# Order of work at the start of expert and mixer stages, and sums of squares folded over blocks before TensorE

## The chip, the cores and the metric

The kernel runs on one core of a Trainium2 chip. The metric is the device time of one execution in microseconds (us), here of the one core's program; the time before is the median of three runs. Engines are named as in the profile: PE (TensorE products; PEld its weight loads), DVE (VectorE), ACT (ScalarE), POOL (GpSimd), SP (SyncE). Each engine runs its own queue of instructions, and waits for others by semaphores. A suffix "q" (ACTq, SPq) marks an instruction that only issues a DMA.

## The reference

A model of four layers on 1,024 tokens of width 256, taken as two batches of 512. Each layer is half a feed-forward part, a mixing part, and half a feed-forward part again:

```python
x = x + 0.5 * ffn(layernorm(x))
x = x + attn(layernorm(x))
x = x + 0.5 * ffn(layernorm(x))
```

The feed-forward parts of layers 0 and 3 are mixtures of experts (32 experts with 6 per token, and 8 experts with 2 per token). Cut to what matters:

```python
scores = softmax(x @ router.T)            # layer 3: sigmoid
w, idx = top_k(scores, K); w = w / (sum(w) + 1e-20)
ye  = (silu(xe @ w_gate) * (xe @ w_up)) @ w_down     # xe: an expert's tokens
y   = sum over the K chosen experts of w * ye
sh  = (silu(x @ ws_gate) * (x @ ws_up)) @ ws_down    # shared expert
return y + sh
```

The mixing parts of layers 2 and 3 are selective state-space mixers (8 heads and 64 heads of width 64, a state of 128, a short convolution of 4 taps):

```python
z, xBC, dt = split(x @ in_proj)
x, B, C = split(silu(conv4(xBC)))
dt = softplus(dt + dt_bias); dA = dt * -exp(A_log)
y[t] = sum_{s<=t} C[t].B[s] * exp(cum[t]-cum[s]) * dt[s] * x[s] + D * x[t]
y = y * silu(z)
y = y * rsqrt(mean(y*y) + eps) * norm_w
return y @ out_proj
```

## The kernel before, in words

The program runs ten stages one after the other: l0_ffn, l0_attn, l0_ffn, l1, l2_ffn, l2_attn, l2_ffn, l3_ffn, l3_attn, l3_ffn. The running x stays in SBUF, tokens on the partitions, 8 chunks of 128 tokens, 4 (CB) to a batch. The order on each engine is set at build time by a scheduler, which takes the program's instructions, their dependencies and its own estimates; `in_order` (L135) chains the instructions traced inside it, engine by engine, so that the listed engines keep the written order. `evac` (L126) copies PSUM to SBUF alternately on DVE (L130) and ACT (L132).

**A MoE stage** (`moe`, four calls: layer 0 twice, layer 3 twice). For each batch: `layernorm` (xn, L223 on DVE), the rows of xn to a table in HBM by a DMA that ACT issues (L652), eight transposes on PE (L177) whose results are evacuated into xT. Then `logits` (ps_lg L317 on PE, lg L320 on DVE), the scores (softmax in layer 0, L728; sigmoid in layer 3, L744), `topk` on DVE (L299 to L309; tk_gt L309 is the mask) and `slot_lists` (L413 on): running sums over tokens by PE (ps_pos L427, L428, from sl_pre and tk_gt), sl_full (L437), sl_v (L441), integer pieces (sl_vi, sl_hl), two one-hot arrays (sl_ol, sl_oh, L459 and L465), their 64 small products (ps_sl L473), a transposition (ps_slt L493), and sl_put and sl_get (L502, L503): for every slot of every expert, which row it takes. A second DMA of ACT puts the weights of the tokens in the table (L672). Traced after this, and allowed on PE only after the logits, is the shared expert (`shared_unit` L354): per batch, two blocks of gate and up products (pg, pu, L365), s = silu (ACT, L368), h = s * pu (DVE, L369), 16 products acc (L375), two additions to x (DVE, L393). The in_order of the front names PE alone.

`experts_sparse` then goes over the units (an expert with up to two tiles of 128 slots): gathers by POOL (L527, table rows at sl_get; four units ahead), `turn_x` (4 transposes, 2 for one tile, L541, evacuated as xeT), `hidden` (ps_gu L551, silu se L555 on ACT, he L556 on DVE), `turn_h` (L565), `down_` (ps_ye L576), and an indirect write of the rows by POOL (L581). In each pass n of its loop (L607 to L620) it traces turn_x(n), turn_h(n-2), hidden(n-1), down_(n-2), so at the start turn_x(0), turn_x(1), hidden(0).

**A mixer stage** (`mamba`; layer 2 has one group of 8 heads, layer 3 has eight). A unit is a batch and a group; a step is one of its four chunks. For a unit there are four blocks of 128 channels: `conv` makes pp on PE (L1675), scales it on ACT (L1678), and gives back its taps (three DVE instructions, L1682) and its SiLU (ACT, L1686) as separate parts; `prep_back` transposes the block (pt L1757) and evacuates it (xt L1758). For a chunk, lm holds the decays of all heads: a DMA brings rows in, `exponents` adds terms on DVE (8 instructions, L1785), `raised` takes one Exp over two chunks on ACT (L1790), `masked` multiplies by the mask M (DVE, L1794). `z_gate` is pz on PE and its SiLU (L1809, L1817), `main` is py on PE (L1837), `gate` is y on DVE and POOL (L1863, L1864), `squares` adds y*y into sqs, 128 channels x 4 blocks x 128 tokens to a chunk (ACT L1871, in later groups ACT L1874 and POOL L1875), `project` is yacc on PE (L1882), `new_state` is pst on PE (L1852) with ACT or DVE (L1854, L1856). When a batch is through, `add_row` sums the squares over channels with products against a column of ones (pr L1896: for each of the 4 chunks, 4 blocks accumulated; the profile counts 32 because each fp32 product stands in two passes), takes rs on ACT and DVE (L156, L157), and adds yacc times rs to x (L1907). For the first batch this falls between the first step of the second batch and its new_state; for the second it ends the stage. ACT needs another table for Exp, Ln, SiLU and Sqrt.

The mixer's start (from about L1950) is an order written out by hand under in_order for PE, ACT and DVE: batch 0's layernorm, decays (`decay_sums`, a generator whose parts are taken with next; d0 and d1 for the two batches: Exp and Ln of dt, dA, jb), the convolutions, the four blocks x[0] to x[3] (x[i][0]() is the taps, x[i][1]() the SiLU), the first exponents and the first Exp, and then the loop over steps. In layer 2 (`few`) batch 1's layernorm and decays stand in the start; in layer 3 they are spread over the first steps.

Of the kernel before, what the change touches and what calls it, by code (L numbers as in the profile page):

```python
# [83 lines left out]
class Net:  # L84
# [421 lines left out]
    def experts_sparse(self, ew, ps, xes, table, rows, lists, w, ex, f, tiles, per, ahead=4, wp=None):  # L506
# [100 lines left out]
        for n in range(N + 2):  # L607
            if n + ahead < N:
                fetch(n + ahead)
            if n < N:  # L610
                st[n].append(turn_x(n, st[n][1], len(units[n][1])))
            if 0 <= n - 2 < N:
                st[n - 2].append(turn_h(n - 2, st[n - 2][3], len(units[n - 2][1])))
            if 0 <= n - 1 < N:
                (wgu, _), xe, xeT = st[n - 1][:3]
                e, js = units[n - 1]
                st[n - 1].append(hidden(n - 1, e, xe, xeT, wgu, len(js)))
            if 0 <= n - 2 < N:
                down_(n - 2, *units[n - 2], st[n - 2][4], st[n - 2][0][1])
                del st[n - 2]  # L620

    def moe(self, pre, names, E, F, K, FS, PER, tiles, cap, r, scores, scale):
# [6 lines left out]
        with ExitStack() as es:  # L629
            lists = es.enter_context(tc.tile_pool(name="f0li", bufs=1))  # L630
            table = self.dram.tile([T, RW], F32, name=f"table{self.calls}")
            rows = self.dram.tile([r * T, D], F32, name=f"rows{self.calls}")
            rv = rows.rearrange("(c p n) d -> c p n d", p=P, n=r)
            xes = [lists.tile([P, 2, RW], F32, name=f"xe{i}") for i in range(6)]
            for t in xes:
                nc.gpsimd.memset(t, 0.0)
            with ExitStack() as fs:
                psA = fs.enter_context(tc.tile_pool(name="f0a", bufs=2, space=PSUM))
                psM = fs.enter_context(tc.tile_pool(name="f0m", bufs=4, space=PSUM))
                psL = fs.enter_context(tc.tile_pool(name="f0l", bufs=2, space=PSUM))  # L640
                xT = fs.enter_context(tc.tile_pool(name="xT", bufs=1)).tile([P, KD, T], F32, name="xT")
                work = fs.enter_context(tc.tile_pool(name="f0w", bufs=2))
                sb = fs.enter_context(tc.tile_pool(name="f0", bufs=1))
                with tc.tile_pool(name="ln", bufs=1) as lp:
                    tv = table[:, :D].rearrange("(b c p) d -> b p c d", p=P, b=B)
                    rT = self.router_weights(sb, psM, router, E)
                    tail = {}
                    with self.in_order(tail, ("PE",)):
                        for b in range(B):
                            xn = lp.tile([P, CB, D], F32, name=f"xn{b}")  # L650
                            self.layernorm(lp, xn, b, *self.scales(lp, b))
                            nc.scalar.dma_start(tv[b], xn)  # L652
                            for k in range(KD):
                                self.transpose_tokens(xn, xT, psM, b, k)
                        s = self.logits(sb, psM, xT, rT, E)
                if cap < T:

                    zero = lists.tile([P, D], F32, name="zero")
                    nc.vector.memset(zero, 0.0)
                    for c in range(NC):  # L660
                        nc.gpsimd.dma_start(rv[c, :, :K, :], zero.unsqueeze(1).to_broadcast([P, K, D]))
                m = sb.tile([P, NC], F32, name="m")
                scores(s, m)
                mask = self.topk(sb, s, E, K)
                get, put, full = self.slot_lists(lists, sb, psL, mask, E, PER * P, cap, r)
                nc.vector.tensor_tensor(s, s, mask, ALU.mult)
                nc.vector.tensor_reduce(m, s, AX.X, ALU.add)
                nc.vector.tensor_scalar(m, m, 1e-20, None, ALU.add)
                nc.vector.reciprocal(m, m)
                nc.vector.tensor_scalar(m, m, scale, None, ALU.mult)  # L670
                nc.vector.tensor_tensor(s, s, m.unsqueeze(2).to_broadcast([P, NC, E]), ALU.mult)
                nc.scalar.dma_start(table[:, D:].rearrange("(c p) e -> p c e", p=P), s)  # L672
                blocks = self.load_shared(sg, su, sd, FS)
                with tc.issue_after(tail["PE"]):
                    for half in range(B):
                        self.shared_unit(work, psA, psM, xT, blocks, half, 0.5)
                over = lists.tile([1, 1], I32, name="over")
                nc.vector.tensor_scalar(over, full[0:1, :], float(len(tiles) * P), None, ALU.is_gt)
            ew = es.enter_context(tc.tile_pool(name="f0e", bufs=1))
            with tc.tile_pool(name="f0p", bufs=1, space=PSUM) as psE:  # L680
                self.puts = []
                args = (table, rows, (get, put), (wg, wu, wd), list(range(E)), F)
                self.experts_sparse(ew, psE, xes, *args, tiles, PER)
            self.prepare_next()
            with tc.tile_pool(name="f0q", bufs=1, space=PSUM) as psE:
                some = nc.values_load(over[0:1, 0:1], min_val=0, max_val=1)
                wp = es.enter_context(tc.tile_pool(name="f0o", bufs=3))
                with tc.If(some > 0):
                    rest = list(range(len(tiles), -(-cap // P)))
                    self.experts_sparse(ew, psE, xes, *args, rest, PER, ahead=0, wp=wp)  # L690
# [871 lines left out]
    def mamba(self, pre, win, wout, nh):  # L1562
# [14 lines left out]
        with ExitStack() as es:  # L1577
# [166 lines left out]
            def prep_front(u, m):  # L1744
                wo, g = u["wo"], u["g"]
                taps, silu = conv(u["wx"][:, :, m * P : (m + 1) * P], g * NM + m, u["b"], u["xc"][:, m, :])

                def rest():
                    nc.scalar.mul(wo[:, m, :], wo[:, m, :], nw[:, g * NM + m : g * NM + m + 1])
                    silu()  # L1750

                return taps, rest
# [27 lines left out]
            def exponents(k):  # L1780


                for h in range(HG):
                    n = k["u"]["g"] * HG + h
                    nc.vector.scalar_tensor_tensor(  # L1785
                        k["lm"][:, h, :], k["lm"][:, h, :], jb[:, k["c"], n : n + 1], top, ALU.add, ALU.min
                    )
# [78 lines left out]
            def squares(k):  # L1866
# [5 lines left out]
                else:  # L1872
                    sq = wk.tile([P, GC], F32, tag="sq", name="sq")
                    nc.scalar.activation(sq, yf, AF.Square)  # L1874
                    nc.gpsimd.tensor_tensor(sqs[:, cc, :], sqs[:, cc, :], sq, ALU.add)  # L1875

            yacc = [psA.tile([P, 2, D], F32, name=f"yacc{i}") for i in range(CB // 2)]

            def project(k):
# [11 lines left out]
            def add_row(b):  # L1891

                pr = psM.tile([P, CB], F32, tag="mm", name="pr")
                for cc in range(CB):
                    for m in range(NM):
                        nc.tensor.matmul(  # L1896
                            pr[:, cc : cc + 1],
                            sqs[:, cc, m * P : (m + 1) * P],
                            self.ones[:, 0:1],
                            start=(m == 0),  # L1900
                            stop=(m == NM - 1),
                        )
                rs = wk.tile([P, CB], F32, tag="rs", name="rs")
                self.rsqrt(rs, pr, scale=1.0 / DI)
                for cc in range(CB):
                    xc = self.x[:, b * CB + cc, :]
                    nc.vector.scalar_tensor_tensor(  # L1907
                        xc, yacc[cc // 2][:, cc % 2, :], rs[:, cc : cc + 1], xc, ALU.mult, ALU.add
                    )
# [27 lines left out]
            with self.in_order(tail, ("PE", "Activation", "DVE")):  # L1937
# [36 lines left out]
                x[1][1]()  # L1974
                x.append(prep_front(us[0], 2))
                prep_back(us[0], 0)
                exponents(ks[0])
                x[2][0]()
                x[2][1]()
                prep_back(us[0], 1)  # L1980
                x.append(prep_front(us[0], 3))
                exponents(ks[1])
                x[3][0]()
                if few:
                    next(d1)
                    next(d1)
                raised(ks[0])
                prep_back(us[0], 2)
                if few:
                    next(d1)  # L1990
                x[3][1]()
                back = (us[0], NM - 1)
                if few:
                    later = {0: [d1.__next__, d1.__next__, d1.__next__], 1: [d1.__next__, lambda: next(d1, None)]}
# [6 lines left out]
            for s in range(NS):  # L2001
# [4 lines left out]
                with self.in_order(tail):  # L2006
# [30 lines left out]
                    if cc % 2 == 0 and ahead:  # L2037
                        exponents(ks[s + 2])
                    if s > 0:
                        project(ks.pop(s - 1))  # L2040
                if s > 0 and n and cc == 0 and order[n][1] == 0:
                    add_row(order[n - 1][0])
                with self.in_order(tail):
# [6 lines left out]
                    elif last and cc == CB - 1:  # L2050
                        products(1)
            squares(ks[NS - 1])
            project(ks.pop(NS - 1))
            add_row(B - 1)

# [63 lines left out]
```

## Time and profile before

| | us |
|---|---|
| median of three runs | 2031.36 (2030.21 to 2033.29) |
| the profiled execution | 2029.85 |
| its span | 2028.0 |
| PE busy | 1762.7 |
| DVE busy | 1131.6 |
| POOL busy | 903.5 |
| ACT busy | 800.6 |
| first gather of the four MoE calls (the wait for sl_get L503 ends just before) | 72.6, 497.9, 1204.3, 1935.3 |

How to read it: the span runs from the first to the last instruction of the profiled execution, whose own time is 1.85 us longer. A line of the timeline gives the start, the duration, the engine and line, the operation with its result and operands, the shape, how many instructions are taken together, and in brackets the idle time of the engine before it and what ended it. Rows of one line that follow each other closely are taken together, so a row's duration can overlap that of the next. The slices cut the span into 40 parts of 50.7 us; PEclk is the granted PE clock in tenths. The mean granted clock of the execution was 0.917.

### The profile page before, as it was taken

The numbers are of one execution on the slowest core, as the hardware profiler recorded it, in microseconds if no ns is written. First come the engines' busy times: TensorE is split into PE (matmuls) and PEld (weight loads), VectorE is DVE, ScalarE is ACT, GpSimd is POOL, SyncE is SP. The second block draws the span as 40 slices with busy tenths as digits, with TensorE's granted clock in tenths as the row PEclk, the third lists the DMA queues.
The fourth block names the chain that finished last, engine by engine and source line by source line (L and its number), as shares of the span: only waits on it lengthen the run. The fifth ranks groups of instructions, "written<-read, shape, count | busy, mean of one in ns | idle before, by whom it ended". The sixth has DMA issues, their size and how long they took to land. (4 is left out here: it accounts for less than half of the span.)

```text
span 2028.0 us, 29711 instructions
## 1 busy us (share of the span) xinstructions
PE 1762.7 (87%) x10662; PEld 1259.7 (62%) x10662; DVE 1131.6 (56%) x2657; ACT 800.6 (39%) x1342; POOL 903.5 (45%) x889
## 2 busy tenths in 40 slices
PE   5899769888999678798788989589999899999895
PEld 4677636565777545444465367357777677777564
DVE  4533276217333476556563653578777677777443
ACT  1132224211232144301751013268777677777111
POOL 3477655311777421100240026135657456667253
PEclk8999989889999789889897979689999999999798
DMA  8266440051565500000220013434454444444133
GB/s 310 80 187 189 153 173 12 16 162 33 170 184 172 209 22 1 22 0 17 100 83 22 11 40 97 131 125 156 152 167 146 154 138 154 160 151 130 44 96 95
DMA packets 117441, 226.49 MB, mean 112 GB/s; under 512 B 22383, under 2 KB 68829, under 8 KB 117015
## 3 DMA queue, kind: packets, MB, share of 16 engines
q1 hardware_dynamic: 88134, 170.17, 26.2%
q0 software_dynamic: 20608, 48.45, 7.6%
q10 hardware_dynamic: 8528, 5.72, 0.9%
q8 instruction: 93, 1.52, 0.3%
q14 instruction: 78, 0.63, 0.1%
HBM read 195.59 MB, written 41.81 MB: 117 GB/s over the span
## 5 line engine op out<-in xcount | busy, mean ns | idle before, releaser
L527 POOL DMA_INDIRECT xe<-table,sl_get x176 | 179.9, 1022 | 202.0 <-DVE sl_get L503 148.1
L551 PE MATMUL ps_gu<-we,xeT 128*128 128x352 f32 x704 | 232.5, 472 | 0.0
L581 POOL DMA_INDIRECT rows<-ye,sl_put x176 | 177.0, 1006 | 83.7 <-issue 40.5
L1682 DVE SCALAR_TENSOR_TENSOR xc<-pp,L_attn_cols,xc 128x511 f32<-128x511 f32 (+2 forms) x216 | 161.4, 747 | 34.7 <-ACT xc L1678 29.4
L576 PE MATMUL ps_ye<-we,hT 88*128 88x256 f32 x704 | 168.3, 379 | 2.9 <-ACT ye L132 1.6
L556 DVE SCALAR_TENSOR_TENSOR he<-se,xe,ps_gu 128x176 f32<-128x176 f32 x176 | 69.9, 397 | 180.2 <-ACT se L555 169.1
L551 PEld LDWEIGHTS ps_gu<-we,xeT 128*128 128x128 f32 x704 | 130.0, 196 | 56.5 <-issue 5.5
L576 PEld LDWEIGHTS ps_ye<-we,hT 88*128 88x128 f32 x704 | 133.0, 190 | 37.0 <-ACT ye L132 3.6
L1809 PE MATMUL pz<-xT,wt 128*128 128x128 f32 x1152 | 144.4, 279 | 11.9 <-ACT xt L1758 5.5
L1785 DVE SCALAR_TENSOR_TENSOR lm<-lm,jb,top 128x128 f32<-128x128 f32 x576 | 153.6, 340 | 0.0
L1675 PE MATMUL pp<-xT,wx 128*128 128x512 f32 x288 | 144.9, 628 | 5.6 <-issue 2.4
L1809 PEld LDWEIGHTS pz<-xT,wt 128*128 128x128 f32 x1152 | 137.8, 195 | 17.0 <-issue 9.6
L1882 PE MATMUL yacc<-wt,y 128*128 128x256 f32 x576 | 144.4, 394 | 0.7 <-POOL y L1864 0.7
L1864 POOL TENSOR_TENSOR y<-y,sg 128x512 f32<-128x512 f32 x72 | 91.7, 1274 | 106.8 <-DVE y L1863 105.2
L1802 POOL TENSOR_TENSOR ce<-ce,CT 128x1024 f32<-128x1024 f32 x54 | 127.9, 2369 | 0.0
L1882 PEld LDWEIGHTS yacc<-wt,y 128*128 128x128 f32 x576 | 104.8, 191 | 24.2 <-issue 10.8
L1514 PE MATMUL ps_y<-w8T,xT 128*128 128x512 f32 x256 | 118.9, 619 | 0.0
L555 ACT ACTIVATE se<-ps_gu 128x176 f32<-128x176 f32 x176 | 55.9, 318 | 154.0 <-PE ps_gu L551 153.9
L1837 PE MATMUL py<-lm,xt 128*64 128x128 f32 x1152 | 108.0, 281 | 8.0 <-issue 6.5
L1875 POOL TENSOR_TENSOR sqs<-sqs,sq 128x512 f32<-128x512 f32 x56 | 71.4, 1275 | 89.4 <-ACT sq L1874 89.4
L1794 DVE TENSOR_TENSOR lm<-lm,M 128x1024 f32<-128x1024 f32 x72 | 87.1, 1215 | 42.7 <-ACT lm L1790 41.1
L217 POOL TENSOR_SCALAR ln_rstd<-ln_mv 128x4 f32<-128x4 f32 x15 | 3.5, 236 | 238.2 <-DVE ln_mv L209 227.5
(401 smaller groups left out, 3478.6 us busy)
## 6 DMA issues: line engine op xcount, KB each, us to landing
lm<-rows SPq DMA_DIRECT2D x72, 512.0 KB
ce<-rows SPq DMA_DIRECT2D x54, 512.0 KB
rows<-zero POOLq DMA_DIRECT2D x16, 768.0 KB, 11.8
y<-rows SPq DMA_DIRECT2D x16, 768.0 KB
we<-in_L_ffn_w_gate_dram SPq DMA_DIRECT2D x64, 176.0 KB
we<-in_L_ffn_w_up_dram SPq DMA_DIRECT2D x64, 176.0 KB
we<-in_L_ffn_w_down_dram SPq DMA_DIRECT2D x64, 176.0 KB
we<-in_L_ffn_w_dram SPq DMA_DIRECT2D x48, 176.0 KB
```

Of the source, the lines that this page charges most:

```text
L527: nc.gpsimd.indirect_dma_start(xe[:, i, :], None, table, bass.IndirectOffsetOnAxis(get[:, e * per + j : e * per + j + 1], 0), bounds_check ...
L551: nc.tensor.matmul(pg, xeT[:, k, i * P : (i + 1) * P], wgu[:, :, k], start=(k == 0), stop=(k == KD - 1))
L576: nc.tensor.matmul(py[:, i, :], hT[:, q, i * P : (i + 1) * P], wd[:, q, :], start=(q == 0), stop=(q == 1))
L581: put_rows = nc.gpsimd.indirect_dma_start(rows, bass.IndirectOffsetOnAxis(put[:, e * per + j : e * per + j + 1], 0), y[:, i, :], None, bou ...
L1514: nc.tensor.matmul(ps, xT[:, k, cs], self.w8T[:, k, 2 * e2 : 2 * e2 + 2, :], start=(k == 0), stop=(k == KD - 1))
L1675: nc.tensor.matmul(pp, wv[:, k, :], xT[:, k, b * S : (b + 1) * S], start=(k == 0), stop=(k == KD - 1))
L1682: nc.vector.scalar_tensor_tensor(out[:, 3 - w :], pp[:, : S - 3 + w], cw[:, m, w : w + 1], out[:, 3 - w :], ALU.mult, ALU.add)
L1785: nc.vector.scalar_tensor_tensor(k["lm"][:, h, :], k["lm"][:, h, :], jb[:, k["c"], n : n + 1], top, ALU.add, ALU.min)
L1802: nc.gpsimd.tensor_tensor(k["ce"], k["ce"], ct, ALU.mult)
L1809: nc.tensor.matmul(pz[:, m, :], u["wz"][:, kk, m * P : (m + 1) * P], xT[:, kk, c * P : (c + 1) * P], start=(kk == 0), stop=(kk == KD - 1),)
L1837: nc.tensor.matmul(py[i * HP : (i + 1) * HP, m, :], w[:, h * HP : (h + 1) * HP], v[:, h, :], start=(m == 0 and n == 0), stop=(n == len(src ...
L1882: nc.tensor.matmul(yacc[cc // 2][:, cc % 2, :], k["y"][:, m, :], u["wo"][:, m, :], start=(u["g"] == 0 and m == 0 and cc % 2 == 0), stop=(u ...
```

## The change

It has four parts. (1) In `experts_sparse`, the second unit's turn_x is traced after hidden(0) and not before it. (2) In `moe`, the two DMAs that write xn to the table are issued after the logits, not after each batch's layernorm, and ACT's order is now held too. (3) In the mixers, `all_squares` sums the four blocks of a chunk's squares on DVE in the last group (sqm, 128 x 128 for each chunk; 16 such instructions in all), and add_row takes 4 products per batch for 16. The tile sqm shares the one buffer of tag "cr" with the decays' rows. (4) In the mixers' start, exponents(0) follows the front of x[3], the SiLU of x[3] and prep_back of x[2] precede exponents(1) and the first Exp, and in layer 2 the parts of d1 are taken one before and two after that Exp.

```diff
@@ experts_sparse
-            if n < N:
+            if n < N and n != 1:
                 st[n].append(turn_x(n, st[n][1], len(units[n][1])))
...
                 st[n - 1].append(hidden(n - 1, e, xe, xeT, wgu, len(js)))
+            if n == 1 and n < N:
+                st[n].append(turn_x(n, st[n][1], len(units[n][1])))
@@ moe
-                    tail = {}
-                    with self.in_order(tail, ("PE",)):
+                    tail, xns = {}, []
+                    with self.in_order(tail, ("PE", "Activation")):
                         for b in range(B):
                             xn = lp.tile([P, CB, D], F32, name=f"xn{b}")
                             self.layernorm(lp, xn, b, *self.scales(lp, b))
-                            nc.scalar.dma_start(tv[b], xn)
+                            xns.append(xn)
                             for k in range(KD):
                                 self.transpose_tokens(xn, xT, psM, b, k)
                         s = self.logits(sb, psM, xT, rT, E)
+                        for b in range(B):
+                            nc.scalar.dma_start(tv[b], xns[b])
@@ mamba
+            sqm = {}
+
+            def all_squares(k):
+
+                cc = k["cc"]
+                if k["u"]["g"] == NG - 1:
+                    if cc == 0:
+                        sqm[0] = wk.tile([P, CB, P], F32, tag="cr", name="sqm", bufs=1)
+                    nc.vector.tensor_reduce(
+                        sqm[0][:, cc, :], sqs[:, cc, :].rearrange("p (m t) -> p t m", m=NM), AX.X, ALU.add
+                    )
@@ add_row
                 for cc in range(CB):
-                    for m in range(NM):
-                        nc.tensor.matmul(
-                            pr[:, cc : cc + 1],
-                            sqs[:, cc, m * P : (m + 1) * P],
-                            self.ones[:, 0:1],
-                            start=(m == 0),
-                            stop=(m == NM - 1),
-                        )
+                    nc.tensor.matmul(pr[:, cc : cc + 1], sqm[0][:, cc, :], self.ones[:, 0:1], start=True, stop=True)
@@ the mixer's start
                 x.append(prep_front(us[0], 2))
                 prep_back(us[0], 0)
-                exponents(ks[0])
                 x[2][0]()
                 x[2][1]()
                 prep_back(us[0], 1)
                 x.append(prep_front(us[0], 3))
+                exponents(ks[0])
+                x[3][0]()
+                x[3][1]()
+                prep_back(us[0], 2)
                 exponents(ks[1])
-                x[3][0]()
+                if few:
+                    next(d1)
+                raised(ks[0])
                 if few:
                     next(d1)
                     next(d1)
-                raised(ks[0])
-                prep_back(us[0], 2)
-                if few:
-                    next(d1)
-                x[3][1]()
                 back = (us[0], NM - 1)
@@ the loop over steps, and after it
                     if s > 0:
+                        all_squares(ks[s - 1])
                         project(ks.pop(s - 1))
...
             squares(ks[NS - 1])
+            all_squares(ks[NS - 1])
             project(ks.pop(NS - 1))
             add_row(B - 1)
```

## Prediction

> **What bounds the kernel now.** I read the page's engine sums and slices first, then the costliest groups, then the timelines around each place that the diff touches.
>
> ```profile
> PE 1762.7 (87%) x10662; PEld 1259.7 (62%) x10662; DVE 1131.6 (56%) x2657; ACT 800.6 (39%) x1342; POOL 903.5 (45%) x889
> ...
> PE   5899769888999678798788989589999899999895
> ...
> PEclk8999989889999789889897979689999999999798
> ```
>
> PE is busy for 87% of the span, so a gain has to shorten PE's stream or one of its stalls. The slices show where it is not full: the first two, and the dips around 25 and 30. In the mixers' loops it is full, and there only work taken off PE counts.
>
> ```profile
> L527 POOL DMA_INDIRECT xe<-table,sl_get x176 | 179.9, 1022 | 202.0 <-DVE sl_get L503 148.1
> ```
>
> Gathers begin only when sl_get exists (148.1 of 202.0 us idle). In a MoE stage the chain is logits, mask, slot list, first gather, first expert. The fourth MoE's timeline:
>
> ```profile
> 1917.56 1.88 PE L365 MATMUL pu<-xT,wsh 128*88 128x512 f32 x4
> ...
> 1919.28 0.34 PE L427 MATMUL ps_pos<-sl_pre,cst 128*128 128x72 f32 x2
> ...
> 1919.56 0.68 DVE L369 SCALAR_TENSOR_TENSOR h<-s,pu 88x512 f32<-88x512 f32 x1
> ...
> 1920.16 0.15 DVE L437 TENSOR_REDUCE sl_full<-ps_pos 128x1 f32<-128x8 f32 x1
> ...
> 1921.57 2.29 DVE L459 TENSOR_TENSOR sl_ol<-sl_hl,cst 128x2048 f32<-128x2048 f32 x1
> ...
> 1935.28 0.20 DVE L503 TENSOR_SCALAR sl_get<-sl_put 128x64 int32<-128x64 int32 x1
> 1935.76 1.17 POOL L527 DMA_INDIRECT xe<-table,sl_get  x1 [34.84 <-DVE sl_get L503]
> ...
> 1943.36 3.14 PE L551 MATMUL ps_gu<-we,xeT 128*128 128x352 f32 x5
> ```
>
> One pair of gate and up products has run; ps_pos (L427) follows the second pair; sl_ol starts 1.4 us after sl_full, sl_get ends the list, the gather starts at once, and ps_gu waits until 1943.36, behind ps_xe of both the first and the second expert. Whatever stands earlier on DVE or PE delays this whole row.
>
> Batch boundary of the layer 3 mixer, where add_row's products (pr) run, and the next step's same products:
>
> ```profile
> 1628.59 4.39 PE L1896 MATMUL pr<-cst,sqs 128*128 128x1 f32 x32
> ...
> 1632.84 2.05 PE L1852 MATMUL pst<-xd,Bt 128*128 128x512 f32 x2
> ...
> 1634.68 3.57 PE L1675 MATMUL pp<-xT,wx 128*128 128x512 f32 x4
> ...
> 1644.14 1.02 PE L1852 MATMUL pst<-xd,Bt 128*128 128x512 f32 x2
> ...
> 1645.00 1.88 PE L1675 MATMUL pp<-xT,wx 128*128 128x512 f32 x4
> ```
>
> pr costs 4.39 us, and after it pst takes 2.05 us for 1.02 and pp 3.57 for 1.88: half speed.
>
> Boundary of the layer 2 mixer, and both mixers' fronts:
>
> ```profile
> 1059.68 0.41 DVE L223 TENSOR_SCALAR xn<-x,ln_mv,ln_rstd 128x256 f32<-128x256 f32 x1 [2.57 <-POOL ln_rstd L218]
> 1060.01 2.34 DVE L1794 TENSOR_TENSOR lm<-lm,M 128x1024 f32<-128x1024 f32 x2
> ...
> 1061.32 0.69 PE L1837 MATMUL py<-lm,xt 128*64 128x128 f32 x4 [4.17 <-issue]
> ```
>
> ```profile
> 992.76 0.71 PEld L1757 LDWEIGHTS pt<-cst,xc 128*128 128x128 f32 x4 [8.65 <-ACT xc L1686]
> ```
>
> ```profile
> 1336.89 0.72 PEld L1757 LDWEIGHTS pt<-cst,xc 128*128 128x128 f32 x4 [6.79 <-ACT xc L1686]
> ```
>
> First MoE, ACT's queue ahead of the logits:
>
> ```profile
> 22.59 1.28 ACT L132 ACT_TABLE_LOAD   x1 [22.59 <-DMA we<-in_L_ffn_w_down_dram]
> ...
> 24.52 3.49 PEld L317 LDWEIGHTS ps_lg<-routerT,xT 128*128 128x128 f32 x16 [4.08 <-ACT xT L132]
> ...
> 27.81 0.37 ACTq L652 DMA_DIRECT2D table<-xn  x1
> ```
>
> PE waits 3.97 us for an evacuation by ACT, whose queue stood behind an issue.
>
> At 1061.32 py waits for lm, which stands on DVE behind xn, itself waiting 2.57 us for POOL. In the fronts PE stands 7.08 and 5.96 us for a SiLU, held behind an Exp and its tables.
>
> **What the Trainium skill says.** "TensorE: Matmul & The Clock Gate", section "What's actually happening": the array runs at half clock after an idle window and recovers after a busy one. The trace agrees in size (1.02 to 2.05 us); here one-column products count as idleness. Same page, "Architectural detail": ScalarE's and VectorE's queues are strict FIFO. The trace agrees: lm at 1060.01 follows xn. "VectorE: DVE Perf Modes", section "The perf-mode tier table": a reduce has the 1x mode only; the trace's nearest, y L1863 with 512 elements, takes 0.69 us, and I price the new reduce at that. "ScalarE: Activation LUTs", "What ACT_TABLE_LOAD costs": 1.283 us a load; the trace has 1.28.
>
> **The change, part by part** (minus is faster; the order of instructions per engine is read from the compiled programs).
>
> *Second expert's transposes behind hidden(0), four MoE calls.* ps_gu(0) needs only its own xeT, ready at 1941.29 + 0.69 = 1941.98 instead of 1943.36. I take -1.2 in each layer 3 call; in layer 0 ps_gu(0) could start at 79.3 instead of 81.26, but he and turn_h then stand behind the second transposes, and ye moves only from 88.77 to about 88.1: -0.6. Sum -3.6. The loops after it are PE-bound, so the shift arrives at the end.
>
> *Table's xn rows issued behind the logits.* In the second layer 0 and the layer 3 calls they are issued in 0.37 us each beside ACT idleness: 0. In the first MoE, ACT's second issue (27.81) waits for a queue that an expert weight holds; logits' evacuation behind it waits too (PE 3.97 us at 24.52, 0.71 at 28.86). Logits then end about 5 us earlier, at 27, but the softmax's Exp now stands behind both issues, and the second waits for a weight landing near 34.4, where the Exp ran at 33.46. Bounds -3.4 (slot free earlier) to +1.5; I take -0.2.
>
> *Side effect: the scheduler's order in the MoE fronts moves,* though no line of it is edited. In layer 3 the second h (L369), which needs the second pu, now precedes tk_gt (L309): tk_gt goes from 1916.98 to pu's end 1919.44 + h 0.68 = about 1920.2. On PE a third pg (0.86) and five acc (0.46 each) then precede ps_pos, so sl_full goes from 1920.16 to 1923.4: +3.2. Two x additions (0.67 each, L393) enter before sl_ol: +1.4; one leaves between sl_oh's halves, -0.6; an h replaces it there, +0.65; another addition precedes sl_get, +0.7. Together +5.3 per layer 3 call, below by at most the acc products that fit DVE's waits (+3), above by cold acc products (+8). In the second layer 0 call three acc (1.38 us) before ps_pos and one addition give +2.2. Sum +12.8. First layer 0: contained in the -0.2.
>
> *Squares added over blocks, then 4 products for 16.* Ends: layer 3's pr is 1886.67 to 1890.3; after: last squares 1886.79, a reduce 0.69, one product 0.25, so rs at 1888.0: -2.3. Layer 2's pr is 1075.45 to 1079.68; rs then comes at about 1076.5: -3.2. The 16 reduces (0.69 each, 11 us) lie on DVE, busy 56%, beside PE work. Boundaries: in layer 3 three products run at once and the fourth waits for the reduce, which is behind eight exponents (to 1630.5), so pst goes from 1632.84 to 1631.3, -1.5, and if PE stays warm pst and pp give 1.03 + 1.69 more, up to -4.2. DVE's exponents and the reduce could hold it at 0. I take -3. In layer 2 py (1043.38) follows pr; it becomes ready with lm at 1041.1, -2.3; the next yacc (3.45, again half speed) shrinks by 1.46. The fourth product falls behind the next pz, and lm's masks now precede xn on DVE, so the 4.17 us stall at 1061.32 goes: lm's Exp, behind rs and two table loads, ends near 1053, masks at 1055.4, against 1061.3. Late next is PE. I take -5.9 for the whole boundary (-2.3 to -7.5).
>
> *SiLU before Exp in the fronts.* Layer 2: one Exp (1.91), one table load each way and jb's (0.23) leave the time before the SiLU at 991.99; y (998.05) is then held by taps (2.32), mask and PE: -3.4 (-2 to -5). Layer 3: y (1342.48) is held by DVE's exponents and taps anyway: -0.5 (0 to -1). Two loads less in layer 2. Queued behind the SiLU are the Exp and masks, with 3 us of slack.
>
> Sum: -3.6 - 0.2 + 12.8 - 5.5 - 8.9 - 3.9 = -9.3 us. The profiled execution took 2029.85 us (span 2028.0 plus 1.85), so 2020.5; the median of the runs lies 1.5 above it: 2022.
>
> **The rivals.**
> 1. The MoE fronts cost little: the moved h and additions fill DVE's waits for PE, and the list is late by 1 to 2 us each (sum +4 for +12.8). For it: DVE idles for 3.07 us before the first h. Against: ps_pos is in FIFO order behind acc, with no freedom. Time -18: 2013.
> 2. The boundaries give nothing: the fourth product waits, PE goes cold again, rs and x arrive late. For it: the reduce stands behind exponents and a chain POOL, DVE, PE. Against: both boundaries show PE waiting for pr and its cold tail. -9.3 + 8.9 = -0.4: 2031.
> 3. Slower: the layer 3 slot lists are later than I compute, because PE is at half speed in that stage (the first pg there took 3.69 us for 1.88) and the nine moved acc and pg products cost double. Decides from +10 each (zero), shows from +12; at 13 each the sum is -9.3 + 15.4 = +6: 2037. Against: the second pair already runs at 1.88.
> That the change doesn't do what it says can be left aside: the compiled orders have 4 products for 16 and the moved SiLUs.
>
> **How the numbers follow.** Forecast 0.50, rival 1 0.20, rival 2 0.17, rival 3 0.13. The forecast's own range, from the bounds of fronts and boundaries, is about 2016 to 2028. A measurement of this kernel can tell about 0.2%, 4 us. Faster by more: 0.48 + 0.20 + 0.02 = 0.70; within: 0.02 + 0.13 + 0.01 = 0.16; slower: 0.02 + 0.12 = 0.14. The range reaches rival 1 and past rival 2: 2012 to 2034.
>
> **What would show it.** In the profile after: ps_gu's first in layer 3 later by about 4 relative to its logits (fronts right) or by none (rival 1); pr with 4 products at each boundary and pp after it at 1.88 (gain) or at 3.57 with a wait for the reduce (rival 2); y's start in the layer 2 front 3.4 earlier; py's 4.17 us stall gone; in the first MoE the Exp near 34.5 behind the second xn issue. I am wrong if the fronts' +5.3 is missing or doubled, or if the layer 2 boundary, the largest single gain, keeps its stall in another place.

## The result, and the profile after

The changed kernel takes 2019.84 us (median of 4 runs, 2017.35 to 2021.04) against 2031.45 us (4 runs, 2030.21 to 2033.29) before: ratio 0.994, 95% interval 0.9923 to 0.9958. The forecast was 2022. The profiled execution has a span of 2016.9 us against 2028.0, so 11.1 us less.

The page of the kernel after, its engine sums, slices and gathers (columns as before):

```profile
PE 1748.0 (87%) x10566; PEld 1243.7 (62%) x10566; DVE 1145.4 (57%) x2673; ACT 796.8 (40%) x1340; POOL 903.6 (45%) x889
...
PE   6899769788999678789788989589999899999885
...
PEclk9899989888999889979897989699999999999788
...
L527 POOL DMA_INDIRECT xe<-table,sl_get x176 | 180.3, 1024 | 211.1 <-DVE sl_get L503 122.0
```

PE has 14.7 us less to do and the span is 11.1 us shorter. The gathers' idle time has grown from 202.0 to 211.1 us: POOL waits longer before the first gathers although the whole became shorter. (The four times given for the first gathers before the change are the starts of sl_get; the gather follows each some 0.5 us later.) That is the side effect in the MoE fronts, to be seen in the timeline of the fourth call after:

```profile
1902.93 1.88 PE L365 MATMUL pu<-xT,wsh 128*88 128x512 f32 x4
...
1904.93 0.68 DVE L369 SCALAR_TENSOR_TENSOR h<-s,pu 88x512 f32<-88x512 f32 x1 [2.61 <-PE pu L365]
...
1905.51 2.32 PE L375 MATMUL acc<-wsh,h 88*128 88x256 f32 x10
...
1907.67 0.34 PE L427 MATMUL ps_pos<-sl_pre,cst 128*128 128x72 f32 x2
...
1908.27 0.17 DVE L437 TENSOR_REDUCE sl_full<-ps_pos 128x1 f32<-128x8 f32 x1
...
1908.75 0.69 DVE L393 TENSOR_TENSOR x<-x,acc 128x512 f32<-128x512 f32 x1
...
1909.62 0.69 DVE L393 TENSOR_TENSOR x<-x,acc 128x512 f32<-128x512 f32 x1
...
1910.81 2.29 DVE L459 TENSOR_TENSOR sl_ol<-sl_hl,cst 128x2048 f32<-128x2048 f32 x1
...
1924.87 0.19 DVE L503 TENSOR_SCALAR sl_get<-sl_put 128x64 int32<-128x64 int32 x1
...
1925.35 1.17 POOL L527 DMA_INDIRECT xe<-table,sl_get  x1 [38.45 <-DVE sl_get L503]
...
1932.13 4.97 PE L551 MATMUL ps_gu<-we,xeT 128*128 128x352 f32 x8 [0.78 <-DVE xeT L130]
```

h (L369) stands right behind the second pu, ten passes of acc stand before ps_pos, and two x additions of 0.69 us each stand between sl_full and sl_ol. The logits arrived on DVE (L320) at 1896.36, so sl_full comes 11.9 us behind them where it came 9.8, sl_get 28.5 us where it came 24.9.

The batch boundary of the layer 3 mixer after, timeline:

```profile
1620.59 0.73 PE L1911 MATMUL pr<-cst,sqm 128*128 128x1 f32 x6
...
1621.17 1.10 PE L1856 MATMUL pst<-xd,Bt 128*128 128x512 f32 x2
...
1622.12 1.88 PE L1679 MATMUL pp<-xT,wx 128*128 128x512 f32 x4
...
1626.24 0.28 PE L1911 MATMUL pr<-cst,sqm 128*128 128x1 f32 x2
```

Three products (6 passes) instead of 16, then pst in 1.10 us (2.05 before) and pp in 1.88 (3.57): full clock. The fourth product (1626.24) is not waited for: it stands in the midst of pz.

Layer 2's boundary and the two mixer starts after, timeline:

```profile
987.34 0.91 PE L1761 MATMUL pt<-cst,xc 128*128 128x128 f32 x4
...
1053.27 2.35 DVE L1798 TENSOR_TENSOR lm<-lm,M 128x1024 f32<-128x1024 f32 x2
...
1054.59 0.44 PE L1841 MATMUL py<-lm,xt 128*64 128x128 f32 x4 [0.43 <-PE pz L1813]
...
1329.89 1.98 PE L1841 MATMUL py<-lm,xt 128*64 128x128 f32 x16 [3.04 <-DVE lm L1798]
```

py at 1054.59 follows lm's mask with 0.43 us of idle time, where it had waited 4.17. In layer 2's start PE takes the transposes at 987.34 without a wait. In layer 3's start a wait of 3.04 us for lm has taken the place of the 5.96 us for a SiLU.

The first MoE call after, ACT's queue:

```profile
27.97 6.17 ACTq L659 DMA_DIRECT2D table<-xn  x2
...
34.19 0.42 ACT L732 ACTIVATE lg<-lg 128x256 f32<-128x256 f32 x1 [13.00 <-DMA we<-in_L_ffn_w_down_dram]
```

The row takes both issues of xn together: the first starts at 27.97, the second only at 33.78, and the softmax's Exp behind them runs at 34.19, although its logits were there 4.8 us earlier than before (27.27 for 32.09).

By stretch of this pair of profiles, the one before the change and the one after it, in us, after against before, each stretch measured from the event that opens it:

| stretch | forecast | measured |
|---|---|---|
| first call, to the end of its expert loop | -0.8 | -1.2 |
| second call: logits to sl_get / sl_get to first ps_ye | +2.2 / -0.6 | +3.7 / -0.8 |
| third call: the same | +5.3 / -1.2 | +3.5 / +1.2 |
| fourth call: the same | +5.3 / -1.2 | +3.6 / -0.4 |
| layer 2 mixer: start / boundary / end | -3.4 / -5.9 / -3.2 | -3.7 / -5.8 / -3.3 |
| layer 3 mixer: start / boundary / end | -0.5 / -3 / -2.3 | 0.0 / -2.6 / -2.0 |
| logits of the third call, at another clock | none | -3.2 |
| sum | -9.3 | -11.0 |

### The profile page after: what moved, and what is told of

The parts are those of the page before. It is cut to its first block, busy times and chain, and to the rows that moved or that the text cites. A ratio compares the mean times of both kernels' runs of the same rounds, so it can differ in the third digit from the quotient of the medians.

```text
span 2016.9 us, 29547 instructions
## 1 busy us (share of the span) xinstructions
PE 1748.0 (87%) x10566; PEld 1243.7 (62%) x10566; DVE 1145.4 (57%) x2673; ACT 796.8 (40%) x1340; POOL 903.6 (45%) x889
## 5 line engine op out<-in xcount | busy, mean ns | idle before, releaser
L527 POOL DMA_INDIRECT xe<-table,sl_get x176 | 180.3, 1024 | 211.1 <-DVE sl_get L503 122.0
L1898 PEld LDWEIGHTS yacc<-wt,y 128*128 128x128 f32 x576 | 104.0, 190 | 23.7 <-issue 10.1
```

Source lines behind the costliest of these rows:

```text
L527: nc.gpsimd.indirect_dma_start(xe[:, i, :], None, table, bass.IndirectOffsetOnAxis(get[:, e * per + j : e * per + j + 1], 0), bounds_check ...
L1898: nc.tensor.matmul(yacc[cc // 2][:, cc % 2, :], k["y"][:, m, :], u["wo"][:, m, :], start=(u["g"] == 0 and m == 0 and cc % 2 == 0), stop=(u ...
```

## The experiments

They ran in three groups, each beside runs of the kernel before on its own chip. On the chips of the first and third group the kernel before took 2120 and 2121 us. The profiles taken there show where the time goes: from the first to the last ps_ye a call of layer 0 takes 186 to 197 us for 154.6, and a call of layer 3 takes 64 to 71 for 55.9. So a run's total is compared within its group, by ratio, and stretches by their own profile. The theory: the issues behind the logits alone move the scheduler's order in the MoE fronts, and cost about 10 us; the folded squares give about 14, by PE's own time, its clock and the masks; the reordered start and the moved transposes give little. Rivals: the late lists are chance or another part's doing; the mixers' gain comes from elsewhere.

**The MoE fronts: whose is the loss?** Without the part, all others kept:

```diff
-                    with self.in_order(tail, ("PE", "Activation")):
+                    with self.in_order(tail, ("PE",)):
...
+                            nc.scalar.dma_start(tv[b], xn)
...
-                        for b in range(B):
-                            nc.scalar.dma_start(tv[b], xns[b])
```

> The changed kernel with the MoE front as before (table rows issued after each batch's layernorm, only PE ordered); the other three parts stay. Theory: the issues behind the logits change the scheduler's order in the MoE fronts and cost +3.7, +3.5 and +3.6 us in calls 2 to 4 (from logits to sl_get, after against before), and give 1.2 us in call 1. Without them: about 2019.8 - 10.8 + 1.2 = 2010 us, ratio 0.990 to the kernel before, and sl_get stands 24.9 us (not 28.5) behind lg in call 4. Rival, the late lists are chance or come from another part: 2018 to 2021, ratio 0.994.

2104.24 us beside 2120.17, ratio 0.9914 (0.9887 to 0.9941). sl_get comes 40.5, 24.1 and 23.7 us behind the logits in calls 2 to 4. Its timeline in the fourth call, where the logits arrived at 1976.91:

```profile
1985.24 0.34 PE L427 MATMUL ps_pos<-sl_pre,cst 128*128 128x72 f32 x2
...
1986.12 0.15 DVE L437 TENSOR_REDUCE sl_full<-ps_pos 128x1 f32<-128x8 f32 x1
...
1987.53 2.29 DVE L459 TENSOR_TENSOR sl_ol<-sl_hl,cst 128x2048 f32<-128x2048 f32 x1
...
2000.62 0.20 DVE L503 TENSOR_SCALAR sl_get<-sl_put 128x64 int32<-128x64 int32 x1
```

ps_pos follows the second pu with no acc before it, sl_full comes 9.2 us behind the logits, and no x addition stands before sl_ol.

The part alone, on the kernel before:

> The kernel before with the MoE front's part alone. Theory: +3.7 + 3.5 + 3.6 - 1.2 = +9.6 us, 2041 us, ratio 1.0047. Rival, it does nothing by itself: ratio 1.000; or it gains by the logits that come 4.8 us earlier in call 1: below 1.000.

2132.62 us, ratio 1.0049 (1.0033 to 1.0065): slower alone, by the size expected. sl_get is 42.6, 29.5 and 29.0 us behind the logits in calls 2 to 4. The theory holds on both sides, and the rival of chance falls. The part consists of two edits, the later issues and the order now held on ACT; no run separates them, so which of the two moves the other engines' order is not shown.

The part in the first call only (the list of engines and the place of the issues depend on the call's number):

```diff
+                            if self.calls > 1:
+                                nc.scalar.dma_start(tv[b], xn)
...
-                        for b in range(B):
+                        for b in range(B if self.calls == 1 else 0):
                             nc.scalar.dma_start(tv[b], xns[b])
```

> The changed kernel with the MoE front's part in the first call only; calls 2 to 4 issue the rows as before, and their scheduler order is then that of the kernel before. Theory: -10.8 us against the changed kernel (sl_get 40.5, 24.5 and 24.3 us behind lg in calls 2 to 4), 1.2 us better than without that part altogether: 2009 us on the first chip, ratio 0.989. Rival: the first call's gain is lost in its expert loop, ratio that of the version without the part.

2009.19 us beside 2029.93, ratio 0.9883 (0.9861 to 0.9904), the fastest of all. sl_get comes 40.5, 24.8 and 24.9 us behind the logits in calls 2 to 4, as in the kernel before. In the same group the changed kernel itself:

> The changed kernel once more, for comparison with the others of this group on the same chip. Ratio 0.994 as before (0.992 to 0.996); rs of layer 3's end 28 us behind the first y of the batch boundary's step as in the first profile. If the gain of the first comparison was chance of the clock, 0.997 or more.

2020.04 us, ratio 0.9944 (0.9926 to 0.9961): the first result again, and the two intervals lie apart. Once more in the third group, as its base:

> The version with the MoE front's part in the first call only, once more, as the base of this group. Ratio to the kernel before 0.988 to 0.990.

0.9921 (0.9899 to 0.9944), above what was expected, and an interval that overlaps that of the changed kernel, which did not run on this chip. sl_get comes as early as in the other group (40.8, 24.4 and 23.9 us behind the logits). Whether the longer expert loops of this chip take up part of what the fronts give is not shown.

**The folded squares.** The part alone, on the kernel before:

> The kernel before with the squares added over blocks alone. Theory: two ends -3.3 and -2.0, two boundaries -5.8 and -2.6, so -13.7 us: 2017.7 us, ratio 0.9932. Rival, part of the layer 2 boundary's gain is that of the reordered start: -10 or less, ratio above 0.995.

2104.95 us beside 2120.17, ratio 0.9927 (0.9904 to 0.9949). Layer 2 from first to last y 66.5 us (73.4 before), both ends -3.3 and -2.0. The layer 3 step of the boundary takes 11.81 us for 14.76. So the gain at the ends and boundaries is this part's own, and needs none of the others.

PE's time or something else? Each product made four times over, reduces kept:

```diff
                 for cc in range(CB):
-                    nc.tensor.matmul(pr[:, cc : cc + 1], sqm[0][:, cc, :], self.ones[:, 0:1], start=True, stop=True)
+                    for _ in range(NM):
+                        nc.tensor.matmul(pr[:, cc : cc + 1], sqm[0][:, cc, :], self.ones[:, 0:1], start=True, stop=True)
```

> The changed kernel, with each of the four products of add_row made four times over (same value each time), so 16 products per batch on PE as before and all the reduces kept. Theory: the number of products is what costs, by their own time and by the half clock behind them: ends +2.7 each, layer 3 boundary +2 for products and up to +2.7 for pst and pp at half clock, layer 2 boundary +2 to +4: +9 to +13 us against the changed kernel, ratio to the kernel before 0.999. Rival, the gain comes from the moved masks and exponents and not from PE: +3 or less, ratio 0.995.

2030.10 us beside 2029.93 (ratio 0.9993, 0.9981 to 1.0004), 10.1 above the changed kernel of the group. By profile the ends are 2.7 and 2.0 us longer, the boundaries 1.5 and 2.0, together 8.2. The part had given 13.7 by the first pair of profiles, so the number of products carries about 8 of these 14 us. At the boundary of layer 2 it carries only 1.5 of 5.8, and there the rival, the moved masks, is right for the larger share. With 16 products too the mask goes ahead of xn on DVE:

```profile
1053.18 2.32 DVE L1798 TENSOR_TENSOR lm<-lm,M 128x1024 f32<-128x1024 f32 x2
...
1058.74 2.32 DVE L223 TENSOR_SCALAR xn<-x,ln_mv,ln_rstd 128x256 f32<-128x256 f32 x4 [0.61 <-POOL ln_rstd L218]
```

The step that had waited for the mask takes 6.67 us, for 6.45 in the changed kernel and 12.23 before: these 5.8 us come with the order on DVE, and not from the number of products. At the boundary of layer 3 one half of the theory fell:

```profile
1622.64 2.73 PE L1912 MATMUL pr<-cst,sqm 128*128 128x1 f32 x24
...
1625.23 1.10 PE L1856 MATMUL pst<-xd,Bt 128*128 128x512 f32 x2
...
1626.18 1.88 PE L1679 MATMUL pp<-xT,wx 128*128 128x512 f32 x4
```

24 passes of one column in 2.73 us, and behind them pst and pp at full clock. With each product six times over, so that 36 passes stand together:

```diff
-                    for _ in range(NM):
+                    for _ in range(6):
```

> The changed kernel, each of add_row's four products made six times over (same value), so that 18 of one column run in one go (36 passes, about 4.1 us) at a boundary where the version with 16 ran 12 in one go (24 passes, 2.73 us) and PE kept its clock. Theory: a run of one-column products of some 3.6 us or more costs the clock: pst 2.05 us and pp 3.57 us behind them in layer 3, the boundary's step 11.8 + 3.4 + 2.7 = 17.9 us. Rival, the clock did not fall for these products: pst 1.10, pp 1.88, step 15.2 us.

```profile
1712.04 4.08 PE L1912 MATMUL pr<-cst,sqm 128*128 128x1 f32 x36
...
1715.98 1.10 PE L1856 MATMUL pst<-xd,Bt 128*128 128x512 f32 x2
...
1716.92 3.31 PE L1679 MATMUL pp<-xT,wx 128*128 128x512 f32 x4
```

This kernel ran once only. Behind 4.08 us of such products pst still takes 1.10 us, but pp 3.31 for 1.88, and the boundary's step takes 17.35 us. The kernel before shows the same in layer 2, where 32 passes took 3.63 us:

```profile
1039.82 3.63 PE L1896 MATMUL pr<-cst,sqs 128*128 128x1 f32 x32
...
1044.59 3.45 PE L1882 MATMUL yacc<-wt,y 128*128 128x256 f32 x8
```

yacc takes 3.45 us there and 1.99 behind the 24 passes (2.74 us) of the same boundary in the version with 16. So in these runs the clock was kept behind 24 passes, at both boundaries, and lost behind 32 or 36, or within them: at 0.113 us a pass, 32 take 3.63, and the 4.39 us in layer 3 before the change mean that the clock fell before the run was through.

Do the reduces cost? In the group of the version with the front's part in the first call only, each reduce behind new_state:

```diff
                     if s > 0:
-                        all_squares(ks[s - 1])
-                        project(ks.pop(s - 1))
+                        done = ks.pop(s - 1)
+                        if cc == 0:
+                            all_squares(done)
+                        project(done)
...
                     new_state(k)
+                    if s > 0 and cc > 0:
+                        all_squares(done)
```

> The version with the front's part in the first call only, and each reduce of squares traced behind the step's new_state and not ahead of it (the last of a batch stays ahead of add_row). Theory: in layer 2 the second and third step after the first y take 15.8 and 8.5 us where they took 14.9 and 7.9 without reduces, because state's addition waits behind a reduce of 1.03 us on DVE; behind it they cost nothing: -1 to -1.5 us. Rival: the steps wait for the taps or masks behind the reduce just as well, 0.

2105.75 us, ratio 0.9932 (0.9911 to 0.9952), beside 0.9921 for its base. The two steps took 15.81 and 8.50 us, as in the base (15.79 and 8.48). The rival is right: the place behind state's addition gives nothing in these steps. It costs elsewhere: in layer 3's last steps a reduce now stands ahead of a mask, and the last two steps take 9.15 and 7.66 us for 7.70 and 6.55. That the steps are 0.9 and 0.6 us longer than without reduces stands in every profile with them; which wait carries it was not isolated.

**The reordered mixer start.** Alone, on the kernel before:

> The kernel before with the reordered mixer start alone. The prediction: -3.4 in layer 2 and -0.5 in layer 3, so -3.9. Theory from the traces: -3.7 in layer 2 (first y 120.7 us behind the logits of the stage before, not 124.3), 0 in layer 3, and the 3.2 us by which the logits of the third MoE call end earlier (81.6 us behind those of the stage before, not 84.8), which so far stood in each profile with this part: -6.9 us, ratio 0.9966. Rival for the last: it is the clock's chance, 84.8 here, ratio 0.998.

2025.83 us beside 2029.93, ratio 0.9986 (0.9975 to 0.9997). Layer 2's first y came 120.67 us behind the logits of the stage before, not 124.35, as expected. The step after it then took 14.55 us for 13.16, because pst and pp run at half clock there (1.66 and 3.05 us): from the logits to the second y it is 135.22 for 137.51, so -2.3. Without the folded squares another 1.6 us are lost up to the last y, so -0.6 in all. The third call's logits came at 80.26 here. Over all profiles, the three kernels without the reordered start show 84.75 to 84.80, and of the eleven with it nine show 80.3 to 81.7 and two 84.5 and 84.7. The same kernel, with the front's part in the first call only, shows 84.48 on one chip and 81.04 on another: the products of the logits (ps_lg, 32 passes) take 6.83 us in the one and 3.91 in the other. So both outcomes occur with the same code, and the -3.2 us of the first pair of profiles comes from the clock; whether the reordered start makes the shorter one more likely is open. The ratio stands for -2.8 us; the full -6.9 us (0.9966) lies outside its interval.

**The second expert's transposes.** As before the change, the rest changed:

> The changed kernel with the second expert's transposes ahead of the first expert's products, as before. The prediction's term: the part gives -3.6 us, so this would take 2023.4 us (ratio 0.996). Theory now, from the two traces: the earlier products run at half clock and the second transposes then stand between first and second products, so the part gives nothing: 2018.5 to 2021, ratio 0.994.

2112.09 us beside 2120.17, ratio 0.9953 (0.9927 to 0.9979), not to be told from 0.994, nor from the 0.996 of the prediction's term. And in the version with the front's part in the first call only:

```diff
-            if n < N and n != 1:
+            if n < N:
...
-            if n == 1 and n < N:
-                st[n].append(turn_x(n, st[n][1], len(units[n][1])))
```

> The version with the front's part in the first call only, and the second expert's transposes ahead of the first expert's products as before. The prediction's term: +3.6 us, with +0.6 in each layer 0 call and +1.2 in each layer 3 call. Theory from ten profiles (time from sl_get to the first ps_ye, with against without the part): +1.1 and +1.3 in layer 0, -0.3 and -0.2 in layer 3, sum +1.9 us: not to be told from zero by the median, 0.988 to 0.991.

2104.35 us beside 2121.33, ratio 0.9914 (0.9888 to 0.994), beside 0.9921 with the part: times with such intervals cannot tell 3.6 us from nothing. From sl_get to the first ps_ye, mean of eight profiles with the part and six without: 15.3 and 16.1 us in call 1, 15.7 and 17.1 in call 2, 15.7 and 15.2 in call 3, 15.1 and 14.7 in call 4. So about -0.9, -1.4, +0.5, +0.4; single profiles spread over some 2 us (13.9 to 16.1 without the part in layer 3), so the sign in layer 3 is not shown.

## Why the prediction was right, point by point

- *MoE fronts.* The order was read rightly from the compiled programs, and the places are as forecast: ps_pos behind acc, sl_ol behind the x additions. The term +5.3 was mis-sized and measured +3.5 and +3.6: sl_full moved by 2.0 and 2.1 us where 3.2 was put, and the rest by 1.5 each where 2.1 was put. PE came through the first two pairs some 0.6 us sooner in the fourth call; that DVE's later insertions partly filled waits is likely, but not isolated. The second call's +2.2 was +3.7 in this pair, which is untypical: over all profiles, six with the part in these calls and eight without, the mean distance from logits to sl_get differs by 1.9, 4.1 and 4.4 us. So the three calls give +10.8 in the first pair and +10.4 in the mean, for +12.8. Rival 1 put +4 for all three and is refuted, rival 3 put 10 and more on each layer 3 call and is refuted too.
- *Issues behind the logits, first call.* As forecast: logits 4.8 us earlier, the Exp at 34.19 (34.5). The whole call gave -1.2 where this part and the next one together were put at -0.8.
- *Second expert's transposes.* The forecast -3.6 failed in its layer 3 half. ps_gu did start earlier against sl_get (7.2 and 7.3 us for 8.1), but its eight passes then took 5.06 us in the third call for 3.77, and 4.97 in the fourth for 4.90, so in the fourth they ran slowly before the change too:

```profile
1943.36 4.90 PE L551 MATMUL ps_gu<-we,xeT 128*128 128x352 f32 x8
```

The second transposes and their evacuation now stand between the first and the second expert's products. -1.2 each measured +1.2 and -0.4 in the first pair and +0.5 and +0.4 in the mean over profiles; -0.6 each measured -0.9 and -1.4. That is -1.4 for -3.6. I had moved the start along the path without asking at what clock the products would run, nor what now stood behind them; how much each of the two takes is not isolated.
- *Ends of the mixers.* -3.2 and -2.3 forecast, -3.3 and -2.0 measured. The reduce was priced at 0.69 us, like an addition of 512 elements. The view of its line says otherwise (count, then ns least/median/most):

```profile
L1889 DVE TENSOR_REDUCE sqm<-sqs x16: 1016/1042/1083, 1016.2 to 1874.8; 128x128 f32<-128x512 f32 x16
```

It takes 1.04 us; in layer 3's end it stands last before the fourth product.
- *Boundary of layer 2.* -5.9 forecast, -5.8 measured, partly by luck, because terms cancel: the three steps with the products and the mask give -3.2, -0.5 and -5.8; the reduces, which I had put beside PE's work, cost +0.9, +0.6 and +0.7; the step at half clock behind the new start costs +1.4.
- *Boundary of layer 3.* The step itself 14.76 to 11.81, -2.95 against -3. The mechanism was partly another: the fourth product was put inside pz by the scheduler and waits for nothing, and the clock stays. I had it wait for the reduce until 1631.3. Two steps before it, one step takes 10.30 us for 8.71, with pz at half clock. The windows show the granted clock (busy us and count of PE, PEld, DVE, ACT, POOL, then PEclk, DMA share and GB/s), before and after:

```profile
1614.00:1616.00 2.00, 1.34 (x12) 1.34 (x13) 2.00 (x7) 1.23 (x3) 0.90 (x1) 1.00 0.51 196
1616.00:1618.00 2.00, 2.00 (x31) 1.88 (x31) 1.51 (x3) 1.25 (x3) 0.00 (x0) 1.00 0.04 8
```

```profile
1604.41:1606.41 2.00, 1.35 (x9) 1.35 (x10) 2.00 (x9) 1.22 (x3) 0.89 (x1) 0.84 0.48 185
1606.41:1608.41 2.00, 2.00 (x11) 1.78 (x12) 1.93 (x5) 0.15 (x1) 0.00 (x0) 0.50 0.00 0
```

PE idled 2.29 us ahead of both; in one the clock falls, in the other not. The same kernel with the front's part in the first call only has 10.20 on one chip and 8.70 on another, so both occur with the same code. But the two profiles without any edit of the mixers have 8.71, and of the twelve with one eleven have 10.19 to 10.32. Whether the change makes the longer step likelier, and so costs some 1.6 us here, is open.
- *Start of the mixers.* -3.4 and -0.5 forecast; -3.7 and 0 to the first y, but 1.4 of the first given back in the next step.

Rival 2, that the boundaries give nothing, fell with the first profile. The total was near partly by luck: the fronts' loss was put some 2 us too high, the transposes' gain some 2 us too high as well, and 3.2 us of the first profile come from the clock in a stage whose code is unchanged. Rival 3 counts nine moved products, where the forecast's own term has six, one pg and five acc; the six are what the timeline after shows. In the median, with its interval of some 3.5 us to each side, none of this can be seen.

## What to carry to other kernels

Compare the compiled order of every engine, not only of the lines that the diff touches: here an edit of ACT's issues and order moved DVE's and PE's work in another place, and with it kept out of three of four calls the change was worth 21 us and not 10 on the chip where both ran (0.9883 and 0.9944; 0.9921 on another chip). Products of one column cost PE's time (0.113 us a pass here), and in a long run its clock as well: fold sums on a less busy engine first, and price the fold by its own instruction. When a start is moved forward, ask at which clock it will run, and what was moved behind it.

## What the runs showed of the hardware

Unexpected were three things. A run of one-column fp32 products keeps PE busy in the profile and still lets its clock fall: 24 passes in 2.73 us left the products behind them at full clock, 32 in 3.63 us and 36 in 4.08 us did not. Whether the clock falls in a wait of 2.3 us, or rises within a stretch of small products, differs between executions of the same kernel on two chips (8.70 or 10.20 us for one step, 81.04 or 84.48 for one stretch), so single profiles differ by some 3 us in one place. Two DMA issues on ACT in the first MoE call took 6.17 us from the start of the first to the end of the second, and held up the Exp behind them; the same two take 1.48 us in the third call.
